# Projections drawn in quarters: attention and a gated feed-forward layer on one Trainium2 core

## The chip, the core and the metric

The kernel runs on one core of one Trainium2 chip. The metric is the device time of one execution in microseconds (us). All times below are us unless ns is written. The engines are named as in the profile: PE (TensorE, matrix products), DVE (VectorE), ACT (ScalarE), POOL (GpSimd) and SP (SyncE, which issues most transfers). A transfer is a DMA.

## What is computed

Four sequences (B = 4) of 512 rows and 512 features pass through attention and a gated feed-forward layer, each followed by a sum with its input and a layer norm. The queries have 16 heads of 32 features; all heads share one key and one value head. The feed-forward weights are reduced to -1, 0 and 1 by their mean magnitude before use.

```
q = rotary((x @ Wq + bq) as 16 heads of 32)
k = rotary(x @ Wk + bk);  v = x @ Wv + bv          # one head
scores = q @ k.T / sqrt(32);  attn = softmax(scores)
x = layernorm(x + (attn @ v) @ Wo + bo)
quantize(w) = clip(round(w / (mean(|w|) + 1e-8)), -1, 1)
hidden = sigmoid(x @ quantize(w1).T) * (x @ quantize(w2).T)   # 1408 wide
x = layernorm(x + hidden @ quantize(w3).T)
```

## The kernel before

**The main loop.** Attention is cut into 64 steps (L791): batch b, group c of four heads, tile t of 128 keys; 16 steps make a batch (`PER`). A step, numbered from 0, does on PE: `scores` (L414), eight matmuls into two score buffers `ps` (four of q and k, four that subtract the row maximum, `negm`); `weigh` (L455), four matmuls of the step before into `acc`, and for batch 0 `count` (L464), four into `den`; the row maxima of the step that comes seven later (`LEAD`, L793); and filling. ACT takes the exponentials `es` of the two score buffers. For batches 1 to 3 POOL adds up the exponentials (`total`) instead of `den`.

**Row maxima.** `find_maxima` (L822) lets PE compute scores into `pmax`, and DVE reduces them (`maxima`). In batch 0 this is `row_maxima` (L368), two chunks in one matmul group with 32 rows. In later batches `maximum` (L379) takes chunks of 512 queries: one alone goes to the bank of `den`, two go to a score buffer, and the last one alone to a score buffer while projections last. After the last maxima of a head group, `spread` (L394) transposes them on PE (`pm`), makes `m` on ACT and DVE, and sends them through DRAM (`rows`) into `negm`.

**PSUM.** There are two score buffers (`sc`, each 1024 wide), one bank for `acc`, one for `den`, and two banks with the tag `mm`. The latter serve all the rest: the projections `pk` and `pq`, the transposed values `pv`, `pm`, the mean `pg` of the weights, the output projection `po`, the transposes `pt` and the feed-forward products `gu` and `po`. A new `mm` tile has to wait until its bank was read for the last time.

**Filling.** `Fill` (L742) holds generators that issue PE work piece by piece. Each `yield` gives the piece's length in us; a negative length says that the tile in work isn't finished, so the next piece comes from the same generator. `draw` (L773) takes pieces until the length due, `pace` for each step (L867), is used up. `project_in` (L262) makes the projections of a batch: first keys and values (`pk`), then four tiles of queries (`pq`), each of four matmuls over four chunks `xT` of the input. Each tile is drawn in halves, with a yield after the second matmul (L273, L294). Behind a query tile DVE rotates it (`turn`, L238): `a`, a shuffle, a product and a sum into `q`, the last three reading and writing the PSUM bank. After batch 0 the result goes to DRAM (`qw`, `qp`) and comes back as `qT` and `qr`. `project_out` (L588) is the output projection, also in halves, and after it follow the transposes `pt` and `feed_forward` (L622). Batch 3's `project_in` waits until step 16 (L266). At its end, `project_in` asks for the next two chunks of `xT` (L320).

**Order.** Nearly all instructions are pinned to program order on their engine (L67 to L86), so the order of the Python calls is the order on PE, DVE, ACT, POOL and SP. SP's transfers wait in line like any instruction: one that waits holds all that follow.

**Quantization.** `quantized` (L158) runs beside batch 0 and the first steps of batch 1: ACT sums magnitudes (`junk`), later takes signs (`sgn`), and DVE makes the ternary weights in place (`raw`), which POOL's queue loads and stores. `junk` and `sgn` use the tile tag `th`; from step 17 on `sgn` uses `rot_a`, which has one buffer (L208).

**Warm-up.** Before the loop, six halves are drawn (L851), and then seven maxima are found, with half of the filling between the two pairs of chunks and half behind them (L853 to L857).

The functions that the change touches, and what calls them:

Of the kernel before, what the change touches and what calls it, by code (L numbers as in the profile page):

```python
# [10 lines left out]
F32 = mybir.dt.float32  # L11
F32R = mybir.dt.float32r
BF16 = mybir.dt.bfloat16
# [7 lines left out]
P = 128  # L21
HD = 32
# [6 lines left out]
def postln_block(  # L29
# [22 lines left out]
    W = 512  # L52
# [105 lines left out]
    def quantized():  # L158

        order = ((0, False), (1, False), (0, True), (2, False), (1, True), (2, True))
        jobs = [(m, last, f) for m, last in order for f in range(NF)]

        means = {}
        for n, (m, last) in enumerate(order):
            if not last:
                for k, step in ((2, 0), (6, 1), (10, 2)):
                    means[(n + 1) * NF + k] = (m, step)
        raws, part, row, pg, hi, waiting = {}, {}, {}, {}, {}, []  # L170

        def load(k):
            if k < len(jobs):
                m, _, f = jobs[k]

                tag, bufs = ("wd", 5) if k % 2 else ("wg", 4)
                raws[k] = wp.tile([P, W], F32, tag=tag, name="raw", bufs=bufs)
                pool.dma_start(out=raws[k], in_=wf[m, f])

        def mean(m, step):  # L180
            if step == 0:
                row[m] = small.tile([P, 1], F32, tag="row", name="row")
                dve.tensor_reduce(row[m], part[m], AX.X, ALU.add)
            elif step == 1:
                pg[m] = ps_mm.tile([P, 1], F32, tag="mm", name="pg")
                mm(pg[m], ones, row[m], True, True)
                gamma = small.tile([P, 1], F32, tag="gamma", name="gamma")
                act.activation(gamma, pg[m], AF.Identity, scale=1.0 / (NF * W * P), bias=eps_q)
                row[m] = gamma
            else:  # L190
                hi[m] = small.tile([P, 1], F32, tag="hi", name="hi")
                act.mul(hi[m], row[m], 0.5)

        AHEAD = 4
        for k in range(AHEAD):
            load(k)
        for k, (m, last, f) in enumerate(jobs):
            load(k + AHEAD)
            if k in means:
                mean(*means[k])  # L200
            raw = raws.pop(k)
            if not last:
                if f == 0:
                    part[m] = small.tile([P, NF], F32, tag="part", name="part", bufs=3)
                junk = work.tile([P, W], BF16, tag="th", name="junk")
                act.activation(junk, raw, AF.Abs, accum_out=part[m][:, f : f + 1])
            else:
                if now > PER:  # L208

                    sgn = work.tile([P, W], BF16, tag="rot_a", name="sgn", bufs=1)  # L210
                else:
                    sgn = work.tile([P, W], BF16, tag="th", name="sgn")
                act.activation(sgn, raw, AF.Sign, bias=hi[m])
                dve.scalar_tensor_tensor(raw, raw, hi[m], sgn, ALU.is_gt, ALU.min)
                waiting.append((kept[m][f], raw))
            if len(waiting) > 2 or k + 1 == len(jobs):
                for w, q in waiting[: 1 if k + 1 < len(jobs) else 3]:
                    pool.dma_start(out=w.bitcast(F32), in_=q)
                del waiting[:1]
            yield  # L220
# [17 lines left out]
    def turn(outs, ps, bias, turned, n, apart):  # L238

        a = work.tile([P, T], F32, tag="rot_c", name="a")
        if apart:
            r = work.tile([P, T], F32, tag="rot_a", name="r", bufs=1)
            act.activation(r[0:n], ps[0:n], AF.Identity, bias=bias[0:n])
        dve.scalar_tensor_tensor(a[0:n], ps[0:n], bias[0:n], cos_sb[0:n], ALU.add, ALU.mult)
        if apart:
            yield
            w = work.tile([P, T], F32, tag="rot_b", name="w", bufs=1)
            dve.stream_shuffle(w[0:n], r[0:n], swap)  # L250
            dve.tensor_tensor(w[0:n], w[0:n], sin_sb[0:n], ALU.mult)
        else:
            w = ps
            dve.stream_shuffle(ps[0:n], ps[0:n], swap)
            dve.scalar_tensor_tensor(ps[0:n], ps[0:n], turned[0:n], sin_sb[0:n], ALU.add, ALU.mult)
        for out, rows in outs:

            engine = pool if apart and out.shape[0] == HD else dve
            engine.tensor_tensor(out, a[rows], w[rows], ALU.add)
        yield  # L260

    def project_in(b):  # L262

        s = batches[b]
        n = P - HD
        while now < NC * NT * (b - 2):  # L266
            yield 0

        pk = ps_mm.tile([P, T], F32, tag="mm", name="pk")
        for c in range(NC):  # L270
            mm(pk, wkv_sb[:, c, :], s.xT[c], c == 0, c == NC - 1)
            if c == 1:
                yield -1.8  # L273
        kv = work.tile([P, T], F32, tag="kv", name="kv", bufs=1)
        act.activation(kv, pk, AF.Identity, bias=bkv_sb[:, 0:1])
        s.kT = work.tile([P, T], F32, tag="kT", name="kT", bufs=3)
        rotation = turn(
            [(s.kT[0:n], slice(0, n)), (s.kT[n:P], slice(0, HD))],
            pk, bkv_sb[:, 0:1], bkv_sb[:, 1:2], n, now < 0,
        )  # L280
        next(rotation)
        yield 1.8
        next(rotation, None)
        if b > 0:
            late.append((slot + 2, split_k(b)))
        for c in range(NC):

            while b + 1 == B and c + 2 >= NC and not batches[0].projected:
                yield 0
            pq = ps_mm.tile([P, T], F32, tag="mm", name="pq")  # L290
            for d in range(NC):
                mm(pq, wq_sb[c][:, d, :], s.xT[d], d == 0, d == NC - 1)
                if d == 1:
                    yield -1.8  # L294
            if b == 0:

                if c == 0:
                    room = work.tile([P, NC, T], F32, tag="y0", name="room", bufs=1)
                q = s.q[c] = room[:, c, :]
            else:  # L300
                q = work.tile([P, T], F32, tag="q", name="q")
            rotation = turn(
                [(q, slice(0, P))], pq, bq_sb[:, c : c + 1], bq_sb[:, NC + c : NC + c + 1], P, now < 0
            )
            next(rotation)
            if c == 0:
                pv = ps_mm.tile([P, NT, P], F32, tag="mm", name="pv")
                for t in range(NT):
                    transpose(pv[:, t, :], kv[:, ts(t, P)], ident)
                s.v = work.tile([P, NT, HD], F32, tag="v", name="v", bufs=3)  # L310
                act.copy(s.v, pv[:, :, n:P])
            whole = b > 0 and next(rotation, "end") == "end" if now >= 0 else False
            if whole:
                middle.append((slot, store_q(b, c, q)))
            yield 1.8
            next(rotation, None)
            if b > 0 and not whole:
                late.append((slot + 1, store_q(b, c, q)))
            s.done = c + 1
# [268 lines left out]
    def project_out(b):  # L588
# [4 lines left out]
        for t in range(NT):  # L593
            po = ps_mm.tile([P, D], F32, tag="mm", name="po")
            for c in range(NC):
                mm(po, s.ctxT[c][:, ts(t, P)], wo_sb[:, c, :], c == 0, c == NC - 1)
                if c == 1:
                    yield -1.8
            dve.tensor_tensor(s.x[t], s.x[t], po, ALU.add)
            stats(s.x[t], mv, t)  # L600
            if t == NT - 1:
                late.append((slot + 1, layernorm(s.x, mv)))
                ready = slot + 5
                s.projected = True
            yield 1.8

        while slot < ready or (b and not batches[b - 1].y_done):
            yield 0
# [133 lines left out]
    class Fill:  # L742
# [3 lines left out]

        def __init__(self):
            self.gens, self.urgent, self.due, self.turn, self.open = [], [], 0.0, True, None

        def add(self, gen):  # L750
            self.gens.append(gen)

        def next_of(self, gens):
            while gens:
                length = next(gens[0], None)
                if length is not None:
                    self.open = gens if length < 0 else None
                    return abs(length)
                gens.pop(0)
            return None  # L760

        def one(self):
# [3 lines left out]
            for gens in kinds:  # L766
                length = self.next_of(gens)
                if length:
                    self.turn = gens is self.gens
                    return length  # L770
            return 0

        def draw(self, us, least=False):  # L773

# [73 lines left out]
    fill.add(project_in(0))  # L848
    for b in range(1, B):
        fill.add(project_in(b))  # L850
    for _ in range(6):  # L851
        fill.one()
    for n in range(LEAD):  # L853
        find_maxima(n, 0, 1)
        fill.draw(0.9)
        find_maxima(n, 2, 3)
        fill.draw(0.9)  # L857
        due()
        if n == 0:
            move(wo_sb, wo.rearrange("(c p) m -> p c m", p=P))  # L860
# [3 lines left out]
    last = None  # L864
    for n, (b, c, t) in enumerate(steps):
        now = n
        pace = (1.8, 3.8, 4.8, 4.6)[b]  # L867
        if t == 1 and PER <= n + NT - 1 < len(steps):
            load_q(*steps[n + NT - 1][:2])
        es = scores(b, c, t)  # L870
# [14 lines left out]
                    late.append((slot + 6, load_x(b)))  # L885
        if batches[-1].done < NC:

            if b == 0:
                find_maxima(n + LEAD, 0, 1)
                begin_middle()  # L890
                due()
# [1 line left out]
            else:  # L893
                find_maxima(n + LEAD, 0)
                find_maxima(n + LEAD, 1, 2)
                find_maxima(n + LEAD, 3)
                begin_middle()
                due()
# [83 lines left out]
```

## Time and profile before

| what | value |
|---|---|
| three timed runs | 660.57, 663.16, 663.67 (median 663.16) |
| the profiled execution's own time | 659.87 |
| its span in the profile | 658.1 |
| mean granted PE clock | 0.997 |
| busy share of PE, DVE, ACT, POOL | 97%, 67%, 43%, 50% |
| PE's idle time before `pmax`, waiting for ACT `es` | 1.8 in 5 waits |
| batch 0's steps begin at | 44.29 (step 0), 51.08, 57.56, 63.99, ... 143.12 (step 15) |
| steps 16, 20, 24 and 28 begin at | 149.43, 179.94, 209.34, 238.36 |

A line of the timeline gives the start from the beginning of the span, the length, the engine, the source line, the operation, `out<-in` with the tiles' names, shapes, and how many equal instructions were merged; in brackets it has the idle time of the engine ahead of it and what ended it. Nearly all instructions have the line of a helper (L75, L80, L83), so they are told apart by their tiles. A PE instruction can also be held without an idle time being shown: then its own length is stretched, as the ends of matmuls are modelled.

### The profile page before, as it was taken

What the parts mean: (1) busy time and instruction counts of PE and PEld (TensorE: products, weight loads), DVE (VectorE), ACT (ScalarE), POOL (GpSimd) and SP (SyncE); (2) the same over time, 40 slices, a digit from 0 to 9 for tenths busy, and PEclk for the clock granted to TensorE, in tenths of its full rate; (3) what the DMA queues carried; (4) which work ended last, traced back from release to release, by engine and by line L of the source; (5) the groups of instructions that cost most, each with busy time, mean ns of one, the idle gap of its engine ahead of it and who ended that gap; (6) DMA issues with size and microseconds to landing.
All of it is one profiled execution on the core that took longest, in us unless ns stands there. A gap on an engine that the chain in (4) does not pass through costs nothing.

```text
span 658.1 us, 9358 instructions
## 1 busy us (share of the span) xinstructions
PE 635.4 (97%) x3194; PEld 357.2 (54%) x3194; DVE 440.3 (67%) x629; ACT 282.6 (43%) x441; POOL 327.4 (50%) x416
## 2 busy tenths in 40 slices
PE   8999999999999999999999899999998999999995
PEld 5233333443333356665555566655555685778884
DVE  3987765787998977676666867667536544364335
ACT  2474656564454645333244354333454521234213
POOL 2434344545998766467666275576575703202000
PEclk9999999999999999999999999999999999999998
DMA  8946669788676286464132457541131473237531
GB/s 265 316 164 209 204 194 273 230 254 259 171 238 205 89 250 190 136 191 147 46 106 77 117 163 219 158 143 44 55 116 52 145 236 120 81 112 229 175 109 64
DMA packets 60671, 107.78 MB, mean 164 GB/s; under 512 B 14592, under 2 KB 15360, under 8 KB 60624
## 3 DMA queue, kind: packets, MB, share of 16 engines
q1 hardware_dynamic: 51984, 80.57, 40.2%
q0 software_dynamic: 7920, 25.96, 12.3%
q10 hardware_dynamic: 720, 0.66, 0.4%
q8 instruction: 25, 0.41, 0.3%
q14 instruction: 22, 0.18, 0.1%
HBM read 84.06 MB, written 23.10 MB: 163 GB/s over the span
## 4 chain that ended last, share of the span: by engine, by line
PE 85%; DVE 9%; ACT 4%; issue 2%; POOL 0%; DVEq 0%; ACTq 0%; POOLq 0%
PE gu L80 24%; PE po L80 19%; PE ps L80 13%; PE pmax L80 9%; PE acc L80 7%; PE pq L80 7%; DVE maxima L75 3%; ACT es L75 2%; PE den L80 2%; PE pk L80 2%; DVE part L75 1%; DVE xt L75 1%; DVE y L75 1%; DVE st L75 1%; PE warm L80 1%
## 5 line engine op out<-in xcount | busy, mean ns | idle before, releaser
L75 DVE TENSOR_REDUCE maxima<-pmax 128x1 f32<-128x512 f32 (+1 forms) x169 | 157.8, 955 | 69.9 <-PE pmax L80 69.7
L75 ACT ACTIVATE es<-ps 128x1024 f32<-128x1024 f32 x128 | 124.2, 1021 | 117.6 <-PE ps L80 116.7
L80 PE MATMUL gu<-y,wg 128*128 128x512 f32 x704 | 171.6, 393 | 0.1
L80 PEld LDWEIGHTS gu<-y,wg 128*128 128x128 f32 x704 | 131.7, 188 | 33.7 <-issue 4.9
L75 POOL TENSOR_TENSOR total<-total,es 128x512 f32<-128x512 f32 x96 | 125.2, 1336 | 38.5 <-ACT es L75 38.3
L80 PE MATMUL po<-wd,h 128*128 128x512 f32 x352 | 86.5, 394 | 3.3 <-DVE y L75 2.9
L75 POOL TENSOR_TENSOR total<-es 128x512 f32<-128x512 f32 x48 | 60.9, 1302 | 52.5 <-ACT es L75 52.5
L80 PE MATMUL pmax<-kr,qr 128*128 128x512 f32 x192 | 74.7, 452 | 3.2 <-DVE maxima L75 1.0
L80 PEld LDWEIGHTS po<-wd,h 128*128 128x128 f32 x352 | 65.1, 188 | 20.8 <-DVE y L75 4.6
L75 ACT CAST h<-hw 128x512 fp32r<-128x512 f32 x44 | 27.3, 620 | 103.0 <-DVE hw L75 103.0
L80 PE MATMUL acc<-es,v 128*32 128x512 f32 x512 | 68.2, 605 | 0.0
L80 PEld LDWEIGHTS pmax<-kr,qr 128*128 128x128 f32 x192 | 34.6, 188 | 55.9 <-issue 17.0
L75 DVE SCALAR_TENSOR_TENSOR hw<-th,gu 128x512 f32<-128x512 f32 x44 | 30.2, 686 | 44.3 <-PE gu L80 43.1
L80 PE MATMUL po<-wo_sb,ctxT 128*128 128x512 f32 x128 | 58.8, 592 | 0.0
L75 DVE TENSOR_TENSOR h<-hw,h 128x512 fp32r<-128x512 f32 x44 | 44.2, 1005 | 21.7 <-ACT h L75 21.4
L80 PE MATMUL ps<-negm,ones_r 2*128 2x512 f32 x256 | 58.7, 788 | 0.0
L75 DVE SCALAR_TENSOR_TENSOR xt<-po,xt 128x512 f32<-128x512 f32 x48 | 32.8, 684 | 37.0 <-PE po L80 37.0
L80 PE MATMUL ps<-qT,kT 32*128 32x512 f32 x384 | 56.3, 640 | 0.0
L75 POOL DMA_DIRECT2D raw<-in_wf x66 | 36.0, 548 | 38.1 <-DMA w<-raw 27.2
L80 PE MATMUL pq<-xT,wq_sb 128*128 128x512 f32 x112 | 53.1, 602 | 0.9 <-ACT v L75 0.9
L75 ACT ACTIVATE th<-gu 128x512 f32<-128x512 f32 x44 | 26.3, 597 | 49.9 <-PE gu L80 49.8
L80 PEld LDWEIGHTS po<-wo_sb,ctxT 128*128 128x128 f32 x128 | 24.1, 189 | 21.2 <-issue 19.2
(99 smaller groups left out, 640.2 us busy)
## 6 DMA issues: line engine op xcount, KB each, us to landing
wg<-w SPq DMA_DIRECT2D x88, 256.0 KB
raw<-in_wf POOLq DMA_DIRECT2D x66, 256.0 KB, 4.6
qr<-qp SPq DMA_DIRECT2D x96, 128.0 KB
wd<-w SPq DMA_DIRECT2D x44, 256.0 KB
w<-raw POOLq DMA_DIRECT2D x33, 256.0 KB, 4.6
qp<-q SPq DMA_DIRECT2D x48, 128.0 KB
rden<-flat SPq DMA_DIRECT2D x64, 64.0 KB
xt<-in_x SPq DMA_DIRECT2D x16, 256.0 KB
```

What stands on the lines that cost most here:

```text
L75: return lambda *args, **kw: pin(getattr(self.engine, name)(*args, **kw))
L80: pin(nc.tensor.matmul(out, lhsT=lhsT, rhs=rhs, start=start, stop=stop))
```

## The change

Projections are drawn in quarters. Every matmul of `pk`, `pq` and the output projection is followed by a yield of 0.9, where there was one of 1.8 after two. The length of the six halves ahead of the warm-up becomes twelve quarters, and the warm-up draws once behind both pairs of maxima.

The pace of batch 0 rises from 1.8 to 2.1, and that of steps 16 to 19 falls from 3.8 to 1.4. In step 0 a draw of 1.8 comes ahead of the maxima. Step 16 still takes its maxima in two pairs (`n <= PER`). From step 17 on, while projections last, one quarter can be drawn between the second and the last `pmax` of a step, if the tile in work isn't about to be finished (`quarter`). The gate that kept batch 3's projections until step 16 is removed; `kT` and `v` get four buffers instead of three for that.

Two tiles change their tags: `sgn` always uses `th` (two buffers), and `r`, which `turn` needs in the warm-up, uses `hw` (two buffers) in place of `rot_a` (one).

```diff
@@ quantized
-                if now > PER:
-                    sgn = work.tile([P, W], BF16, tag="rot_a", name="sgn", bufs=1)
-                else:
-                    sgn = work.tile([P, W], BF16, tag="th", name="sgn")
+                sgn = work.tile([P, W], BF16, tag="th", name="sgn")
@@ turn
-            r = work.tile([P, T], F32, tag="rot_a", name="r", bufs=1)
+            r = work.tile([P, T], F32, tag="hw", name="r")
@@ project_in
-        while now < NC * NT * (b - 2):
-            yield 0
...
             mm(pk, wkv_sb[:, c, :], s.xT[c], c == 0, c == NC - 1)
-            if c == 1:
-                yield -1.8
+            if c < NC - 1:
+                yield -0.9
...
-        s.kT = work.tile([P, T], F32, tag="kT", name="kT", bufs=3)
+        s.kT = work.tile([P, T], F32, tag="kT", name="kT", bufs=4)
...
-        yield 1.8
+        yield 0.9
...
                 mm(pq, wq_sb[c][:, d, :], s.xT[d], d == 0, d == NC - 1)
-                if d == 1:
-                    yield -1.8
+                if d < NC - 1:
+                    yield -0.9
...
-                s.v = work.tile([P, NT, HD], F32, tag="v", name="v", bufs=3)
+                s.v = work.tile([P, NT, HD], F32, tag="v", name="v", bufs=4)
...
-            yield 1.8
+            yield 0.9
@@ project_out
-                if c == 1:
-                    yield -1.8
+                if c < NC - 1:
+                    yield -0.9
...
-            yield 1.8
+            yield 0.9
@@ Fill
+            self.pieces = 0
...
                     self.open = gens if length < 0 else None
+                    self.pieces = self.pieces + 1 if length < 0 else 0
...
+        def quarter(self):
+            if self.pieces < NC - 1:
+                self.due -= self.one()
@@ warm-up
-    for _ in range(6):
+    for _ in range(12):
         fill.one()
     for n in range(LEAD):
         find_maxima(n, 0, 1)
-        fill.draw(0.9)
         find_maxima(n, 2, 3)
-        fill.draw(0.9)
+        fill.draw(1.8)
@@ main loop
-        pace = (1.8, 3.8, 4.8, 4.6)[b]
+        pace = (2.1, 3.8, 4.8, 4.6)[b] if n < PER or n >= PER + NT else 1.4
...
-            if b == 0:
+            if n == 0:
+                fill.draw(1.8)
+            if n <= PER:
                 find_maxima(n + LEAD, 0, 1)
...
                 find_maxima(n + LEAD, 1, 2)
+                fill.quarter()
                 find_maxima(n + LEAD, 3)
```

What PE then draws, in quarters (one matmul each; `pk`, `pq` and, from step 20, the output projection):

| steps | before | after |
|---|---|---|
| before the loop | 26 | 26 |
| 0 | 2 | 4, two of them ahead of `pmax` |
| 1 to 15 | 2 each | 2 each, and 3 in steps 2, 5, 8, 11 and 14 |
| 16 to 19 | 4, 4, 4, 2 | 1, 2, 2, 1 |
| 20 to 23 | 4 each | 4, 5, 4, 4 |
| 24 and 25 | 6, 2 | 4, 4 |

Batch 3's `pk` moves from steps 16 and 17 to steps 14 and 15.

## The prediction

> **What bounds the kernel now.** I read the page first: the busy shares, the slices and the chain that ended last.
>
> ```profile
> span 658.1 us, 9358 instructions
> ...
> PE 635.4 (97%) x3194; PEld 357.2 (54%) x3194; DVE 440.3 (67%) x629; ACT 282.6 (43%) x441; POOL 327.4 (50%) x416
> ...
> PE   8999999999999999999999899999998999999995
> ...
> DVE  3987765787998977676666867667536544364335
> ...
> PE 85%; DVE 9%; ACT 4%; issue 2%; POOL 0%; DVEq 0%; ACTq 0%; POOLq 0%
> ...
> raw<-in_wf POOLq DMA_DIRECT2D x66, 256.0 KB, 4.6
> ```
>
> PE is busy almost throughout and carries 85% of the chain. The change adds no matmul, so it can only move PE's waits. Where are they now, and which new ones does the new order make? The PE timeline answers the first, stage by stage; a matmul in f32 is two records, a quarter of a projection is one matmul.
>
> ```profile
> 46.76 2.04 PE L80 MATMUL pmax<-kT,room 32*128 32x512 f32 x8 [1.08 <-ACT es L75]
> ...
> 67.72 1.16 PE L80 MATMUL pmax<-kT,room 32*128 32x512 f32 x8
> 68.81 1.98 PE L80 MATMUL pq<-xT,wq_sb 128*128 128x512 f32 x4
> 70.63 0.28 PE L80 MATMUL pg<-row,ones 128*128 128x1 f32 x2
> ...
> 177.80 0.50 PE L80 MATMUL pmax<-kr,qr 128*128 128x512 f32 x1 [0.19 <-ACT es L75]
> ...
> 229.20 0.66 PE L86 MATMUL pt<-ident,xt 128*128 128x128 f32 x4 [1.13 <-DVE q L75]
> ```
>
> The reader is to see three kinds of waits, and in the last line the kind that matters below: `pt` wanted a `mm` bank that still held a projection, and stood until DVE had written its `q`. The DVE timeline gives the durations.
>
> ```profile
> 50.76 0.75 DVE L75 SCALAR_TENSOR_TENSOR a<-pq,bq_sb,cos_sb 128x512 f32<-128x512 f32 x1 [0.46 <-PE pq L80]
> ...
> 52.95 0.69 DVE L75 TENSOR_TENSOR q<-a,pq 128x512 f32<-128x512 f32 x1
> 53.56 0.74 DVE L75 SCALAR_TENSOR_TENSOR raw<-raw,hi,sgn 128x512 f32<-128x512 f32 x1
> ...
> 68.89 2.36 DVE L75 TENSOR_REDUCE maxima<-pmax 128x2 f32<-128x1024 f32 x2 [0.26 <-PE pmax L80]
> 71.17 1.44 DVE L75 SCALAR_TENSOR_TENSOR raw<-raw,hi,sgn 128x512 f32<-128x512 f32 x2
> ```
>
> Start to start, a rotation takes 53.56 - 50.76 = 2.80, a pair of maxima 71.17 - 68.89 = 2.28 from 1.17 after its `pmax` began, a `raw` 0.67. On PE a quarter is 0.86 (1.72 for two in the chain from step 9 on), the first behind a 32-row `pmax` 0.95.
>
> **What ends.** Step numbers are those of the main loop.
> - Step 0: `pmax` waits 1.08 and is then stretched from 1.14 to 2.04. Two quarters put ahead of it (1.9) cover the exponentials: -2.0.
> - Batch 0, starts of steps: from the first `ps` to `acc` is 1.30 where nothing waits (51.08 to 52.39), and 1.87 at 63.99, because the second score buffer is freed by the second maxima. Over steps 2 to 16 the excess is 6.2. A third quarter in steps 2, 5, 8, 11 and 14, and the longer steps below, remove some 2.9.
> - Step 16: `pmax` idles 0.93 for ACT's `sums`, which held `den`; pairs of chunks no longer use that bank: -0.9.
> - Steps 17 to 25: four `pmax` take 1.04 at 108.21 but 1.50 at 176.64 to 178.14; the excess is 3.6 in nine steps. A quarter ahead of the last chunk covers 3.0 in seven of them; splitting costs 0.1 each (0.34 for a chunk that stands alone against 0.24): -2.3.
> - Smaller waits in steps 20 and 26: -0.5.
>
> Together -8.6.
>
> **What comes.** PE takes its instructions in order, so all that is queued behind a waiting one waits too. The order of the changed program shows these.
> - Step 3: one quarter closes a projection, one opens the next, and then `pg` needs a `mm` bank. Both are taken; the closed one is free when its rotation is done, and on DVE that stands behind the step's two maxima and a `raw`. On the old clock: 71.17 + 0.67 + 2.80 = 74.64 against 70.63: +4.0. Before, no projection closed in this step.
> - Step 5: the same with `pm` and two quarters between: 81.18 + 1.17 + 2.28 + 0.67 + 2.80 = 88.1 against 82.28 + 0.95 + 1.72 = 84.95: +3.2.
> - Step 14: with the gate gone, batch 3's `pk` follows in the same draw in which its third `xT` chunk is first asked for. SP issues it behind `flat` (142.34, 0.34 long), so from 142.7 at the earliest, later if DVE's rotation delays `flat`; PE wants it at 140.17 + 1.04 + 1.72 = 142.9. The nearest row, `raw`, lands 256 KB in 4.6 (2.4 to 7.5): +4.6, bounds 2.2 and 7.3. Before, a whole step lay between.
> - Step 0 to 1: the rotation is now ahead of the maxima on DVE: 47.6 + 0.2 + 2.80 + 2.28 = 52.9, PE is there at 51.0: +1.9. Most of the gain of step 0 goes back.
> - Steps 16 to 20: with one quarter a step is shorter than DVE's part. Step 16: `raw`, the rotation of `pk` (165.32 to 168.91, 3.6), `raw`, maxima: 7.2 against PE's 5.05: +2.2. Steps 18 and 19: maxima end 0.54 + 2.42 after the first `pmax`, PE needs 2.0: +0.9 each. Together +4.0, half of it if DVE runs ahead.
> - Step 21: the next output projection tile takes the bank of `pm`, which is read only behind a rotation, `part` (1.24) and the maxima: 2.80 + 1.24 + 2.42 + 0.27 from the step's start = 6.7, PE is there at about 4.3: +2.4, bounds 0 and 4.6 (a `raw` there has taken 2.96 instead of 0.74 beside POOL's adds).
> - Step 20: `m` moves from early in step 17 to step 18, so `rows`, four `rden` and `negm` on SP have one step less. `rows` to landing was 4.9 once (141.39 + 0.56 to 146.85): 0 to +4.2, I take +1.0.
> - `v` copies right behind `pv` in steps 8 and 17: 0.5 each, less the 0.36 that such a wait cost at 172.43: +0.6.
>
> Sum: 4.0 + 3.2 + 4.6 + 1.9 + 4.0 + 2.4 + 1.0 + 0.6 = 21.7, less 8.6: **+13**. The profiled execution took 659.87 (span 658.1), so 673; it lies 3.3 under the median of the runs, 663.16, so that I forecast 663.2 + 13 = **676**.
>
> **At nothing.** In the warm-up one quarter is drawn a step later; there PE waits for the maxima of the step before anyway (the `pmax` at 20.41 is stretched to 2.09), which hides it; without that 0.9. `r` and `sgn` get two buffers: ACT idled for DVE before some `sgn` (3.68 at 217.45), but each `es` still began 1.4 after its `ps`. Extra `kT` and `v` buffers only allow the early `pk`. Each moved projection takes its `qw` and four `qp` transfers along on SP and a subtraction on POOL; SP stands idle 1.9 at 134.3 and POOL 1.6 at 147.6, so they are covered in batch 0. The 7 moved quarters cost PE in batch 0 what they save later; one `gu` block more is done by step 27 and one less is left at the end.
>
> The rows show a granted clock of 1.00 in every stretch of 10 us up to 650 and no PE idle above 1.5, so nothing here says what an idle time of 4 does. [...]
>
> **Rivals.**
> 1. The fill works (ends on the faster side). Place: the maxima and exponentials that hold PE in steps 0 to 26. DVE was busy only 6.84 of 10 us around 85, so it could finish rotations before PE asks. Price: all that ends, -8.6, hence 654.5. It decides if the new waits stay under 5.3 together. Against it: at steps 3 and 5 the rotation cannot start before the maxima end, whatever DVE's mean load. 5%.
> 2. The three great waits (steps 3, 5, 14) do not hold, since bank and chunk come in time: 676 - 11.8 = 664, no change. For it: I infer these waits from the order. Against it: 229.20 shows such a wait. 8%.
> 3. DVE and SP fall further behind: `raw` beside POOL's adds costs 0.7 more in five steps (3.5), `negm` is late by 3.5 rather than 1: 676 + 6 = 682. For it: the 2.96 row. Against it: long PE waits give DVE time. 22%.
>
> The forecast keeps 65%. Low prices of the open terms (step 14 at 2.2, step 21 and `negm` at 0, steps 16 to 20 halved) give 668; high ones (7.3, 4.6, 4.2) give 684. The range is 667 to 684. About 0.5% (3.3 us) is what a measurement can tell from no change: faster 5%, within it 8%, slower 87%.
>
> **What will show it.** The waits of the changed kernel's PE should list `pg` and `pm` behind `DVE q` with some 4 and 3, `pk` behind `DMA xT` with 2 to 7, and `po` behind `DVE m`; `pmax` behind `ACT es` and `ACT sums` should be gone, and the span should be longer by about what the idle rows add. Right in kind but wrong in size is it if step 14's transfer lands early; wrong it is if PE shows no idle above 1.5 before step 26, or if the time is lost after step 28, where I see only the one `gu` moved.

## The result, and the profile after

The changed kernel takes 689.7 (median of six runs, 687.7 to 692.6), the kernel before on the same chip 663.1 (660.6 to 663.7). The ratio is 1.041 (95% interval 1.038 to 1.044): slower by 26.6, twice the 13 of the forecast and beyond its range. The direction was right; the size was not. Ratios leave out executions more than 1.5% above the fastest of their kernel, but medians don't, so the spread is given where a version's executions lie far apart.

The profiled execution after took 687.9. From its page, the rows that answer to those shown of before:

```profile
span 686.1 us, 9380 instructions
...
PE 645.8 (94%) x3194; PEld 359.2 (52%) x3194; DVE 439.0 (64%) x628; ACT 281.9 (41%) x441; POOL 329.7 (48%) x416
...
PEclk9999889998899999999999999999999999999999
...
PE 80%; DVE 13%; issue 2%; ACT 1%; DMA 1%; DVEq 0%; ACTq 0%
```

The same 3194 PE records take 10.4 longer (645.8 against 635.4), and PE's idle time grows by 17.6. The first is the surprise: no matmul was added. The row PEclk says why. Before, it was 9 in every slice up to the last; here it dips in four slices, all in the first third.

Which waits are there? PE's waits in the whole span (in total, times, longest):

```profile
PE pk L80 <- DMA xT<-in_xT: 6.3, 3, 5.9
PE pg L80 <- DVE q L75: 3.8, 1, 3.8
PE ps L80 <- DVE maxima L75: 3.4, 4, 1.5
PE pm L86 <- DVE q L75: 3.2, 1, 3.2
...
PE gu L80 <- DVE h L75: 2.2, 1, 2.2
...
PE po L80 <- DVE m L75: 1.9, 1, 1.9
...
PE pmax L80 <- ACT es L75: 0.2, 1, 0.2
```

The waits on `pg`, `pm`, `pk` and `po` are the forecast's, with 3.8, 3.2, 5.9 and 1.9 for its 4.0, 3.2, 4.6 and 2.4. `pmax` hardly waits for `es` any more. But a wait is not over when it ends. PE's timeline in step 3, and what follows:

```profile
72.75 1.02 PE L80 MATMUL pq<-xT,wq_sb 128*128 128x512 f32 x2
77.59 0.59 PE L80 MATMUL pg<-row,ones 128*128 128x1 f32 x2 [3.82 <-DVE q L75]
78.10 2.09 PE L80 MATMUL ps<-room,kT 32*128 32x512 f32 x8
79.19 1.43 PE L80 MATMUL ps<-negm,ones_r 2*128 2x512 f32 x4
80.55 1.94 PE L80 MATMUL acc<-es,v 128*32 128x512 f32 x8
82.25 1.33 PE L80 MATMUL den<-es,ones 128*32 128x512 f32 x8
83.51 1.14 PE L80 MATMUL pmax<-kT,room 32*128 32x512 f32 x8
```

`ps` takes 2.09 where it took 1.14, `acc` 1.94 where it took 1.06 (as in the fence of the busy run below). The same stretch by microseconds (length, PE's busy time and records, granted clock, DMA share, GB/s):

```profile
75.00:76.00 1.00, 0.00 (x0) 1.00 0.91 348
76.00:77.00 1.00, 0.00 (x0) 0.51 0.17 66
77.00:78.00 1.00, 0.41 (x2) 0.50 0.00 0
...
81.00:82.00 1.00, 1.00 (x8) 0.50 0.00 0
82.00:83.00 1.00, 1.00 (x12) 0.58 0.00 0
83.00:84.00 1.00, 1.00 (x12) 1.00 0.00 0
```

The clock is halved at 76.0, in the middle of the wait, and comes back at 82.8, 5.25 after PE has work again. Read in the same way, it is halved from 96.5 to 103.3 (behind `pm`), 164.8 to 175.0 (behind `pk`) and 256.9 to 260.3 (two `pt` waits of 1.63 and 0.54 in step 26). PE worked in 5.25, 5.98, 8.71 and 3.42 of these. At half clock half of that time, 11.7, is lost; this is an estimate, and the 10.4 by which the PE records grew are near it.

Where the 28.0 of the span went, from the starts of the steps in both traces (a moved quarter counted at 0.86, the moved `gu` at 1.83):

| stretch | after less before | without moved work | forecast |
|---|---|---|---|
| up to step 0 | +0.8 | +0.8 | 0 |
| steps 0 to 15 | +27.4, 7 quarters more | +21.4: three waits 12.9, clock 10.0, the rest -1.5 | +9.3 |
| steps 16 to 19 | -6.1, 8 quarters less | +0.8 | +2.2 |
| steps 20 to 27 | +5.8, one quarter and one `gu` more | +3.1: clock 1.7 | +1.6 |
| step 28 to the end | +0.2, one `gu` less | +2.0: `gu` waits 2.2 | 0 |

### The profile page after: what moved, and what is told of

Same layout as the page of the kernel before. It is cut to its first block, busy times and chain, and to the rows that moved or that the text cites. A ratio compares the mean times of both kernels' runs of the same rounds, so it can differ in the third digit from the quotient of the medians.

```text
span 686.1 us, 9380 instructions
## 1 busy us (share of the span) xinstructions
PE 645.8 (94%) x3194; PEld 359.2 (52%) x3194; DVE 439.0 (64%) x628; ACT 281.9 (41%) x441; POOL 329.7 (48%) x416
## 4 chain that ended last, share of the span: by engine, by line
PE 80%; DVE 13%; issue 2%; ACT 1%; DMA 1%; DVEq 0%; ACTq 0%
PE gu L80 23%; PE po L80 18%; PE ps L80 13%; PE pmax L80 9%; PE acc L80 8%; PE pq L80 5%; DVE maxima L75 4%; PE den L80 2%; DVE pq L75 1%; DVE part L75 1%; DVE raw L75 1%; PE pk L80 1%; DMA xT<-in_xT 1%; DVE a L75 1%; DVE xt L75 1%
## 5 line engine op out<-in xcount | busy, mean ns | idle before, releaser
L80 PE MATMUL pmax<-kr,qr 128*128 128x512 f32 x192 | 77.1, 464 | 1.5 <-DVE maxima L75 1.3
L80 PE MATMUL acc<-es,v 128*32 128x512 f32 x512 | 70.8, 626 | 0.0
L80 PEld LDWEIGHTS pmax<-kr,qr 128*128 128x128 f32 x192 | 34.9, 189 | 53.3 <-issue 21.4
L80 PE MATMUL po<-wo_sb,ctxT 128*128 128x512 f32 x128 | 60.5, 593 | 1.9 <-DVE m L75 1.9
L80 PE MATMUL ps<-qT,kT 32*128 32x512 f32 x384 | 59.2, 650 | 2.7 <-DVE maxima L75 2.7
L80 PE MATMUL ps<-negm,ones_r 2*128 2x512 f32 x256 | 60.3, 816 | 0.0
L80 PE MATMUL pq<-xT,wq_sb 128*128 128x512 f32 x112 | 54.5, 604 | 0.9 <-ACT v L75 0.9
L75 DVE SCALAR_TENSOR_TENSOR raw<-raw,hi,sgn 128x512 f32<-128x512 f32 x33 | 31.1, 950 | 9.4 <-ACT sgn L75 9.4
```

The costliest lines, as they stand in the source:

```text
L75: return lambda *args, **kw: pin(getattr(self.engine, name)(*args, **kw))
L80: pin(nc.tensor.matmul(out, lhsT=lhsT, rhs=rhs, start=start, stop=stop))
```

## The experiments

The theories: **A**, each long wait costs its idle time and then the time at half clock; **B**, idle time only; **C**, the engines that PE waits for are late anyway, and other waits take over. Later a fourth, **D**, on `raw` and POOL.

### The three waits, one by one

**Batch 3's chunks early.** At the end of batch 1's projections (after L313):

```diff
+        if b == 1:
+            for c in range(2, NC):
+                next(chunks)
+                batches[3].xT.append(xp.tile([P, D], F32, tag="x", name="xT"))
+                move(batches[3].xT[c], xT[3, :, c, :])
```

> The changed kernel (689.7), with batch 3's last two input chunks loaded early into two tiles that are free until batch 1's rows come, so that step 14's third pk matmul has its chunk; the order of PE stays. Theory A (each long wait costs its idle time and then the time at half clock behind it): the idle 5.9 goes and the clock stays at 1.00 in this stretch, which gives back half of the 8.7 us from the end of the wait to the return of the clock, 4.4: 679.4. Theory B (only the idle time counts, the longer matmul rows behind it cost nothing more): 683.8. Theory C (DVE and SP are late in any case, and the next waits take over): 688 or more.

Measured: 680.0 (674.5 to 682.4), ratio 1.026 (1.021 to 1.031). The wait is gone, and the time is that of A, not of B or C. The profiled execution, the slowest of the four, agrees: its steps 14 to 16 take 9.2 less than the changed kernel's, where A says 10.3 and B 5.9.

**The mean later.**

```diff
-            for k, step in ((2, 0), (6, 1), (10, 2)):
+            for k, step in ((2, 0), (7, 1), (10, 2)):
```

> The changed kernel, with the matmul for the mean of the weights (pg) issued one job of the quantization later, so that in step 3 it no longer asks for a bank right behind the projection that closed; in step 4 it stands behind the maxima, when that bank is long free. Theory A: the idle 3.8 and half of the 5.3 us at half clock behind it go, 6.4 together: 683.3. Theory B: 685.9. Theory C: the wait goes to pm in step 5, which grows from 3.2 towards 7, and the time stays at 689.

Measured: 684.4, ratio 1.032 (1.028 to 1.037), between A and B. The stretch itself decides: steps 3 and 4 take 13.1 together where the changed kernel took 19.2, that is 6.0 less, A's 6.4 and not 3.8. `pm` in step 5 still waits 3.16, so C fails. What is missing at the end was given back far away: behind the loop `gu` waits 2.9 here (2.2 there) and the clock is halved for 6.8 at 564.9.

**PE busy in the waits.** The waits stay; added matmuls fill them.

```diff
+    def busy(k):
+        ps = ps_sc.tile([P, 2, T], F32, tag="sc", name="busy")
+        for i in range(k):
+            mm(ps[:, i % 2, :], ones, cos_sb, True, True)
...
+                if now == 3:
+                    busy(4)
                 pg[m] = ps_mm.tile([P, 1], F32, tag="mm", name="pg")
...
+            if b == B - 1 and c == 2:
+                busy(6)
             mm(pk, wkv_sb[:, c, :], s.xT[c], c == 0, c == NC - 1)
...
+        if now == 5:
+            busy(3)
         pm = ps_mm.tile([P, P], F32, tag="mm", name="pm")
```

> The changed kernel with all its waits, but PE works through most of the three long ones: 4, 3 and 6 added matmuls of 512 columns (0.86 each) go into a free score buffer ahead of pg in step 3, pm in step 5 and the third pk matmul of step 14; nobody reads what they make. Theory A: the waits still end when DVE or the transfer lets them, but the clock stays at 1.00, so half of 5.3, 6.0 and 8.7 goes, 10.0: 679.7. Theory B: added work inside waits changes nothing: 689.7. If the added work outlasts a wait or delays the score buffers, the time is up to 3 longer than either.

Measured: 683.4, ratio 1.031 (1.030 to 1.033). PE's timeline in step 3 of this run:

```profile
75.83 3.60 PE L85 MATMUL busy<-cos_sb,ones 128*128 128x512 f32 x8
79.81 0.38 PE L85 MATMUL pg<-row,ones 128*128 128x1 f32 x2 [0.39 <-DVE q L80]
80.12 1.14 PE L85 MATMUL ps<-room,kT 32*128 32x512 f32 x8
80.69 0.81 PE L85 MATMUL ps<-negm,ones_r 2*128 2x512 f32 x4
81.42 1.06 PE L85 MATMUL acc<-es,v 128*32 128x512 f32 x8
```

`pg` comes 3.98 after the last quarter's end (75.83 to 79.81), no earlier than in the changed kernel with its 3.82, but `ps` and `acc` run at full clock (granted 1.00 in each microsecond from 75 to 84, and 1.14 and 1.06 long). It is the clock that stretched them, and work that nobody needs makes the kernel faster. Between the starts of steps 2 and 16 the run gains 9.0 on the changed kernel, of A's 10.0; B's 0 fails. At the end only 6.3 of it is left, since the clock was halved for 3.4 near 55 and near 567, and `gu` waited 3.9 behind the loop.

**None of the three.** The first try moves `pm` of step 5 half a step later (with the edits of the first two runs):

```diff
-            late.insert(0, (slot + (1 if now < 0 else 3), spread(b, c)))
+            late.insert(0, (slot + (1 if now < 0 else 4 if now == 4 else 3), spread(b, c)))
```

> The changed kernel without any of the three waits: batch 3's chunks early, pg one job later, and the pm of step 5 half a step later. Theory A: 12.9 of idle time and 10.0 at half clock go: 666.8. Theory B: 676.8. Theory C (lateness of DVE shows up in other waits): 680 or more.

Measured: 675.8, ratio 1.022 (1.020 to 1.024), not A's 666.8. The edit had a price that I hadn't seen: `negm` became late, `ps` waited 1.79 for it in step 8, and the clock was halved for 3.4 behind it. The second try moves `pm` earlier instead (`2 if now == 4`):

> As the run without any of the three waits, but the pm of step 5 comes half a step earlier instead of later, so that negm isn't late: there ps stood 1.8 for negm in step 8 and the clock was halved for 3.4 behind it. Theory A (idle time and what the clock loses behind it): 675.8 - 1.8 - 1.7 = 672.3. Theory C (other waits take over): 675 or more.

Measured: 667.6 (666.4 to 676.9), ratio 1.0086 (1.0057 to 1.0115), better than expected. In the profiled execution, the fastest of the five, the longest waits in the loop are 1.85 (`po`), 1.63 (`pt`) and 1.55 (`ps`), and the clock never fell before 660. In the first try's it had fallen three times more, behind waits of 1.66 to 2.33, so not all of the difference between the tries is due to `negm`. So of the 26.6, 22 hang on three waits, though these were only 12.9 long. C is out.

Between the starts of steps 2 and 16 this version needs 4.4 more than before for five more quarters (4.3). Yet the third quarter does what it was drawn for: what the stretches from the first `ps` to `acc` take above 1.30 falls from 6.2 to 3.6 over steps 2 to 16. Most of this is spent in steps 5 and 8. In step 5 it is due to this version's own edit, which puts `pm` between the two pairs of maxima. Before, and here:

```profile
81.18 1.17 PE L80 MATMUL pmax<-kT,room 32*128 32x512 f32 x8
82.28 1.98 PE L80 MATMUL pq<-xT,wq_sb 128*128 128x512 f32 x4
```

```profile
84.11 1.13 PE L80 MATMUL pmax<-kT,room 32*128 32x512 f32 x4
85.17 0.33 PE L86 MATMUL pm<-ident,maxima 128*128 128x128 f32 x1
85.43 1.13 PE L80 MATMUL pmax<-kT,room 32*128 32x512 f32 x4
86.49 1.12 PE L80 MATMUL pq<-spare,wq_sb 128*128 128x512 f32 x2
```

The maxima took 1.1 and now take 2.4 with `pm`. In step 8 `pq` waits 0.35 for `v`.

### Parts of the change alone, on the kernel before

**Filling first in step 0.**

```diff
+            if n == 0:
+                fill.draw(1.8)
             if b == 0:
                 find_maxima(n + LEAD, 0, 1)
```

> The kernel before with one change: a draw of 1.8 ahead of the maxima of step 0. The forecast's terms: -2.0 and, since the rotation now stands ahead of the maxima on DVE, +1.9, +0.5 for v in step 9: no change, 663. Rival (the filling covers the exponentials and the rotation runs beside it): 661. All projections end half a tile earlier than before; if that puts a pg or pm behind one that just closed, a wait of 3 and a halved clock would give 667 or more.

Measured: 674.7, ratio 1.019 (1.017 to 1.022). Of the expectations only the last is right in kind (a long wait, 4.42, and a clock halved for 3.4 behind it), and at another place. In steps 0 and 1 it is neutral as forecast (two more quarters, 1.7, and step 2 starts 1.6 later). But all projections now end half a tile earlier, and in step 16 batch 3's `pk` follows within one draw:

```profile
157.65 1.88 PE L80 MATMUL pk<-xT,wkv_sb 128*128 128x512 f32 x4
163.95 3.36 PE L80 MATMUL pk<-xT,wkv_sb 128*128 128x512 f32 x4 [4.42 <-DMA xT<-in_xT]
```

That is the wait of step 14 again, with the gate still in place. So such a wait doesn't need the gate's removal, which only brought it into step 14; it needs a draw that asks for a chunk and wants it at once. To test this, the same with the chunks loaded early:

> The kernel before with the draw ahead of the maxima of step 0 (674.7 alone) and batch 3's last two chunks loaded early. Theory: step 16 waited 4.4 for its third chunk, as step 14 of the changed kernel did, and lost 1.7 at half clock: 668.6. The rest of its loss has another cause: raw took 6.05 at 189.3 and ps then waited 1.8, and the clock was halved twice for 6.8: these stay.

Measured: 668.8, ratio 1.013 (1.009 to 1.018), as expected. The rest is as told: `raw` lasts 6.08, `ps` waits 1.83 behind it, and the clock falls twice, for 3.4 and 6.8.

**Batch 1's part: quarters, pairs in step 16 and the quarter between the maxima.** Pace, gate and step 0 are those of before.

```diff
-            if b == 0:
+            if n <= PER:
                 find_maxima(n + LEAD, 0, 1)
...
                 find_maxima(n + LEAD, 1, 2)
+                fill.quarter()
                 find_maxima(n + LEAD, 3)
```

> The kernel before with quarters, with step 16's maxima in pairs and with the quarter between the maxima of steps 17 to 25; the old pace, the gate for batch 3 and no filling first in step 0. The forecast's own terms: -0.9 in step 16 and -2.3 for the maxima, so 660. Against that, the pairs put the pm of step 17 behind that step's draw, right behind a pk that closed two quarters before: its bank is free after the 3.6 of the rotation, 1.7 of it are covered, so 1.9 of idle time, and by theory A up to 3.4 more if the clock falls: 662 to 665.

Measured: 664.6, ratio 1.0043 (1.0011 to 1.0075). `pm` waits 2.8 for the rotation into `kT` in step 17, and the clock is halved for 6.8: by this trace the gain of the quarter is eaten by where the pairs put `pm`. Without the pairs (`if n < PER`):

> The same without the pairs in step 16, so that the pm of step 17 stays ahead of the draw: only quarters, and one of them between the maxima. The forecast's term: -2.3 to -2.6, hence 660; no wait above 1.5 and the clock at 1.00 throughout. Rival (DVE, which reads the maxima, sets the pace of these steps, so that PE's waits come back elsewhere): 663.

Measured: median 663.7, ratio 0.9988 (0.9947 to 1.0030): no difference that can be told. Its ten executions fall into two groups, five from 658.0 to 660.3 and five from 667.1 to 670.1. The profiled one is of the upper group, and DVE's and POOL's timelines at step 22 show its trouble:

```profile
199.41 5.61 DVE L75 SCALAR_TENSOR_TENSOR raw<-raw,hi,sgn 128x512 f32<-128x512 f32 x1
204.94 2.41 DVE L75 TENSOR_REDUCE maxima<-pmax 128x1 f32<-128x512 f32 x3
```

```profile
198.96 0.55 POOL L75 DMA_DIRECT2D w<-raw  x1
199.52 4.95 POOL L75 TENSOR_TENSOR total<-total,es 128x512 f32<-128x512 f32 x4
204.42 0.56 POOL L75 DMA_DIRECT2D raw<-in_wf  x1
```

A `raw` of 0.74 lasts 5.61, until all four of POOL's adds are done. The maxima queue behind it, `ps` waits 2.93 for them, and the clock is halved for 6.8. This suggests theory **D**: with the steps shortened, `raw` meets the adds at times, and this decides between 660 and 668. Three attempts to take `raw` out of the way followed.

### Theory D, and the search for a faster version

**Quantization done in batch 0** (a third job in steps 2 to 15), with the quarter between, and on the kernel before alone:

```diff
-            quantize(1)
+            quantize(2 if 2 <= n < PER else 1)
             fill.draw(pace)
```

With the quarter:

> The kernel before with quarters and one of them between the maxima of batch 1, as in the run that gave 658 to 670, and with three jobs of the quantization instead of two in steps 2 to 15, so that none is left for batch 1. Theory D: the spread of that run came from raw, which once took 5.61 beside POOL's four adds and held the maxima and with them ps for 2.93, and from the clock that fell behind it; without raw in batch 1 all executions lie at 657 to 661. Rival: a third raw (0.67) in each step of batch 0 makes the rotations late there: 663 or more; or the spread has another source and stays at 10.

Without it:

> The kernel before with only the earlier quantization of the last run. It tells what of that run is due to the quarter: if the quarter between the maxima is worth its 2.3, this one lies that much above the last run. Theory D: here raw has cover behind the longer run of projections, so 661 to 663.

Measured: 669.5, ratio 1.011 (1.008 to 1.014), and 671.6, ratio 1.014 (1.011 to 1.017). The first run's rival was right, and the second missed its 661 to 663: from step 11 on `pmax` waits for `es` up to 3.2 and 2.4, so batch 0 pays more than batch 1 saves. But the two differ in batch 1 as hoped, with no `raw` and a full clock there: from step 17 to step 28 they take 74.6 and 77.9. The quarter between the maxima is worth 3.3; the forecast had 2.3.

**`sgn` and `raw` at the head of the step**, before `scores`, from step 17 on:

```diff
+        if n > PER:
+            quantize(1 if n % 3 else 2)
         es = scores(b, c, t)
...
-            quantize(1)
+            quantize(1 if n <= PER else 0)
             fill.draw(pace)
-            quantize(1 if b == 0 or n % 3 == 0 else 0)
+            quantize(1 if n <= PER else 0)
```

With the quarter:

> The kernel before with quarters, one of them between the maxima, and from step 17 on with raw and its sgn at the head of each step, ahead of scores, when POOL's adds of the step before have ended; the number of jobs stays. Theory D (the spread of 658 to 670 came from raw held by POOL's adds): raw lasts 0.7 to 1.3, no wait above 1.5 in batch 1, all executions at 657 to 662, median 659.5. Rival (the spread has another source, for instance where the clock's windows fall): the spread stays at 10. Rival: sgn at the head delays es, and pmax waits for it: 664.

Without it:

> The kernel before with only raw and sgn at the head of the step from step 17 on; PE's order is that of before. Theory D: raw was never on PE's path in the profiled execution of before, so 661 to 663, with fewer executions above 664. The difference to the last run is then what the quarter between the maxima is worth: 2 to 3.

Measured: 665.3, ratio 1.004 (1.002 to 1.006; executions from 660.3 to 673.0), and 672.8, ratio 1.015 (1.011 to 1.020). No use: on the second, `pmax` waits 8.1 for `es` in all, since a late `sgn` at the head holds ACT. On the first, profiled in its slowest execution, two `raw` still lasted 5.71 together, `ps` waited 3.75 behind them, and a `pk` waited 3.16 for its chunk in step 17.

**`raw` alone at the head of the next step:** `sgn` stays, a list holds what DVE has to do, and it is worked off ahead of `scores`.

```diff
-                dve.scalar_tensor_tensor(raw, raw, hi[m], sgn, ALU.is_gt, ALU.min)
-                waiting.append((kept[m][f], raw))
+                held.append((raw, hi[m], sgn, kept[m][f]))
+                if now <= PER or k + 1 == len(jobs):
+                    ternary()
-            if len(waiting) > 2 or k + 1 == len(jobs):
+            if len(waiting) > (2 if now <= PER else 0) or k + 1 == len(jobs):
...
+        if n > PER:
+            later[0]()
         es = scores(b, c, t)
```

From step 17 on POOL also stores each finished piece of the weights without holding back two.

With the quarter:

> The kernel before with quarters and one of them between the maxima; from step 17 on sgn stays where it was, and DVE's raw comes at the head of the next step, when POOL's adds of the step before have ended and those of this step have not begun. Theory D: raw lasts 0.7 to 1.3, ps waits for no maxima above 1.5, pmax waits for no es; all executions at 657 to 662, median 659.5. Rival: the spread has another source and stays at 658 to 670, or raw meets POOL's adds here too.

Without it:

> The kernel before with only raw moved to the head of the next step from step 17 on. Theory D: raw had cover in before, so 661 to 664, no change; the last run lies 2 to 3 below it, which is what the quarter between the maxima is worth.

Measured: 667.0, ratio 1.0073 (1.0047 to 1.0098), and 668.7, ratio 1.0072 (1.0047 to 1.0097). With the quarter a `raw` lasts 5.23 here too (at 189.9, and `ps` waits 2.92 behind it): POOL's adds run into the next step. Without it, `raw` stays at 1.6 at most from step 17 on, but `pmax` waits 7.6 for `es` in all. That a long `raw` is held by POOL is inferred from its rows: each of the eleven above 2.9 in all profiles ends 0.6 behind the end of a POOL operation on tiles, with POOL at work all the while. That this alone makes the two groups of 658 and 668 is not settled, since no version lost `raw` and kept the rest: the one without `raw` in batch 1 (666.4 to 670.5) had changed batch 0.

**Without the three waits, and with the old pace** (the second try above, and the pace 3.8 in steps 16 to 19), and then with `sgn` and `raw` at the head:

The pace:

> As the last run without the three waits (667.6), and with the old pace in steps 16 to 19, so that these steps are longer on PE than on DVE, the output projection is drawn in whole tiles and no gu is drawn ahead of step 28. Theory A (what is left over 663 are the smaller waits that the short steps make): ps 1.55 in step 17, po 1.85 in step 21, ps 1.43 in step 26 and gu 2.5 behind the loop go, up to 7.3: 661. Rival (these waits belong to the quarter between the maxima and not to the pace): 666 to 668.

With `raw` at the head as well:

> The run without the three waits and with the old pace (669.4), with raw at the head of the step from step 17 on. There two raw lasted 6.44 until POOL's adds ended, ps waited 1.77 and 1.73 in steps 18 and 20, and the clock was halved twice for 6.8. Theory D: these go, 3.5 and half of 13.6: 660. Rival (the waits come from the order of rotations and maxima): 667 or more.

Measured: 669.4, ratio 1.009 (1.006 to 1.012), and 666.3, ratio 1.007 (1.004 to 1.010). The waits that were to go went (`gu` behind the loop and `po` in step 21 are gone), but `ps` waits 1.8 and 1.7 behind two `raw` that last 6.44 together, and the clock falls three times for 6.8. At the head of the step one lasts 3.0 and two together 3.3, and a `ps` wait of 3.4 is left. No version beat the kernel before by more than can be told.

## Why the prediction was right and wrong

- **Failed: the after-effect of the waits, which has no term in the sum.** The prediction said that the rows show no clock below 1.00 and no idle above 1.5, so that nothing there says what an idle time of 4 does, and the sum counts each wait at its length alone. The clock fell four times, behind 3.82, 3.16, 5.88 and the pair of 1.63 and 0.54, for 6.8, 6.8, 10.2 and 3.4. At half of the time that PE worked in them, an estimate, this cost 2.6, 3.0, 4.4 and 1.7, together 11.7 of the 15 by which the sum was short of the 28.0. The other 3.3 are waits 1.1 longer than their terms, `gu` at the end 2.0, gains in steps 0 to 15 that came out 1.0 smaller, 0.8 ahead of step 0, less 1.6 in steps 16 to 27. A wait of 4 wasn't needed for a fall: the clock was down 2.3 after PE had gone idle in steps 3 and 5, and 19 of 29 waits of 1.6 to 2.6 brought a fall too (last section).
- **Right: the long waits.** `pg`, `pm` and `po` lie within 0.6 of their terms. `pk` at 5.88 lies within its bounds of 2.2 and 7.3, but 1.3 above the value taken (by the prediction's own numbers, 142.7 + 4.6 - 142.9, this should have been 4.4 and not 4.6). The runs moved each cause (bank, bank, chunk) and the wait went with it. The removed gate put the chunk's wait into step 14, but a wait of this kind doesn't need it: with the gate and the filling of step 0 alone, it came in step 16.
- **About right, but hardly seen in the time: the gain of 2.9 at the starts of batch 0's steps.** The excess of 6.2 fell to 3.6 without the three waits and to 3.4 with PE busy in them. But without the waits, steps 2 to 16 cost no less than their quarters, since steps 5 and 8 took most of it back. In the changed kernel, what steps 0 to 15 show besides the three waits and the clock is -1.5, where the prediction's terms (-2.0, -2.9, +1.9 and +0.5) make -2.5.
- **Right: step 0.** It won about 1.8 and lost it from the start of step 1 on (`ps` idles 0.70 there and is stretched to 1.83).
- **Too high: steps 16 to 20.** +4.0 with the gains of these steps made 2.2 up to step 19; measured 0.8.
- **Missed: "one `gu` block more is done by step 27 and one less is left at the end", costed at nothing.** It isn't returned: `gu` then waits 2.2 behind the loop. All six profiled versions with the early `gu` wait there for 2.2 to 3.9, the other five of them for the transfer of `wg`, and those without it don't wait there. No run changed this alone.
- **Missed: the warm-up, put at nothing with "without that 0.9".** Step 0 begins 0.8 later. This is a tendency only: over the profiles it begins at 44.3 to 45.3 with the old warm-up and at 44.5 to 46.6 with the new.
- **Under-sized: the quarter between the maxima**, 3.3 for 2.3, measured only between two versions without `raw` in batch 1, one profile each.

## What to carry to other kernels

Here a wait on PE had a price list with a step: waits below 1.6 mostly cost their length, and waits above 2.7 nearly always (the clock fell near 17 of 18) their length and some 1.7 to 4.4 more, estimated at half of PE's time at half clock. So one edit that brings a wait of 3 outweighs many that save 0.3 each, and where a long wait can't be avoided, useless matmuls in it can be better than none (683.4 against 689.7). Before a projection is moved, look at what its last quarter meets: who takes the bank that it holds next, and whether its next input was asked for a whole step earlier.

## What the runs showed of the hardware

- **The granted clock changed on a grid of 3.413.** In 17 of the 19 profiled executions the clock fell before 640. Each halved stretch there lasts 3.41, 6.82 or 10.24, and within an execution all of them begin at multiples of 3.413 from each other (76.02, 96.50, 164.76 and 256.92 after the change: 6, 20 and 27 steps of it apart). Cut along this grid, 38 of the 47 falls between 42 and 640 follow a piece in which PE idled for 46 to 100%; seven pieces at full clock with 46 to 57% weren't followed by one. The other nine falls follow pieces with 16 to 40%, and no run shows their cause. So what a wait of 1.6 to 2.6 costs seems to depend on where the grid lies, which differs from one profiled execution to the next: near 19 of 29 such waits the clock fell, and near 17 of the 18 above 2.7. This is my inference, and no run changed the grid's place alone. It would also spread one program's executions: before had 659 to 666, at mean clocks of 0.998 to 0.989, mostly the longer the lower the clock, though one took 664.2 at 0.998.
- **A `raw` on DVE lasted through several POOL instructions.** In five profiles a `raw` of 0.74 (two inputs in SBUF) lasted 5.05 to 6.08 beside four adds in a row (in the timelines of step 22 above from 199.41 to 205.02, the adds from 199.52 to 204.47), whereas the steps of rotations (one input in PSUM) beside such adds kept their 0.69 to 0.76. Not every `raw` is held: of 102 that began while an add ran, 16 took less than 1.0, and no run shows what tells these from the others.
